# The opening of a GRU kernel: biases by repeating transfers, the first weights in halves, the first x sums on VectorE, and the first pair's products in a held order

## The chip, the cores and the metric

One Trainium2 chip, one core. Times are device microseconds (us); three runs of the kernel before give a median of 2737.33 (2737.08 to 2738.55). One further execution was profiled: 2741.09 us, of which the profile's span is 2739.3. Engines are named as in the profile: PE is TensorE's matmuls, PEld its loading of the stationary operand, DVE is VectorE, ACT is ScalarE, POOL is GpSimd, SP is SyncE, which here only issues transfers.

## What is computed

The input x is 128 rows (batch) by 64 time steps by 512 features, `cond` is 128 by 512. All is float32.

```
gi = x[:, t] @ W_ih + b_ih ;  gh = h @ W_hh + b_hh        # 512 x 1536: groups r, z, n
r = sigmoid(i_r + h_r) ; z = sigmoid(i_z + h_z) ; n = tanh(i_n + r * h_n)
h = (1 - z) * n + z * h                                    # h starts as cond
x = x + h @ (sign-quantized W_ffn).T + b_ffn               # signs scaled by mean |W_ffn|
x = x + moe(conv(x, taps = cond) + b_conv)                 # 64 experts, top 6, and a shared one
```

The change concerns the opening of the first two of these lines; everything behind the 64 recurrent steps is the same in both kernels.

## The kernel before

**Input gates.** `gi` doesn't depend on h, so it is made ahead, two time steps (a *pair*) and 512 output columns (a *group* c: 0 is r, 1 is z, 2 is n) at a time. `input_gates` goes over pairs t = 0, 2, 4, ... and in each over the groups in the order 0, 2, 1. A pair and a group make a `Chunk`. The 2 x 2 block product of a chunk (two steps and two halves of the contraction, two halves by two halves of the weights) is made with seven half-size products, n = 1 to 7, from sums of the blocks instead of eight. Each is two float32 matmuls with 256 columns, and so four rows of the profile (x4, two passes each). Their order in the stream is 1, 6, 7, (3 of the chunk before), 2, 4, 5. Four PSUM banks hold them: psx for 1 and then 2, psy for 6, psw for 7 and then 4, psz for 5 and then 3. After each product VectorE reads the bank (L313 to L327) and adds the parts and the bias `bi`; the bank's next product waits for that.

**Operands.** On the weights' side `prepare(c)` makes four block sums on VectorE, once for each group: t1 (L252), t2 (L254), a difference in place (L255) and t4 (L257). Product 1 needs the first half of the contraction rows of the weight block `wih[c]`, product 6 needs t2, which is made from t1 and the second half. On the input's side `pair_operands(t)` makes four sums of 128 x 256 on GpSimd (L269 to L272) from the pair's tile `xp`.

**Biases.** `b_ih` and `b_hh` come as single rows of 6 KB, laid into spare corners of two later buffers (`xc0`, `tzs[0]`). `spread` (L232) copies a row to all partitions: a matmul with a single row of ones as the stationary operand (L236), for b_ih and b_hh one after the other into one bank, psf, and a ScalarE copy out (L239). `prepare` calls it for each group, and `spread(bhn, ...)` at L403 for the recurrent bias of n. In all six matmuls (twelve rows) and four copies.

**Transfers.** SP issues, in this order: xp of the first pair (L197), the two bias rows (L211, L213), the weight block of group 0 (L215, 1 MB as one transfer), h, the blocks of groups 2 and 1, the three recurrent blocks `whh` (L221), the two repeated rows fb and cb (L222, L223, each a 2 KB row sent to 128 partitions), zero rows, the sign weights' source wf (L408). GpSimd's queue issues the pair t = 2 (L218) and every step's x rows xn (L194); in between are its clearing of the buffer `tzs[0]` (L116) and the sums.

**Recurrence.** The driver takes 24 products off the stream, transposes h (L351, copied out by ScalarE at L357), and makes the signs: sum of |wf| (L411, L415), a matmul that adds over partitions (L417), scale and thresholds (L418 to L422), four times two operations for the signs (L427, L428). Then each step t issues the twelve recurrent matmuls psgh (L441, three groups of four, in the order r, n, z), the gates on VectorE and ScalarE (L448 to L462), the output product of the step before (L375, needs the signs), and 10 or 11 products of the stream, which fill PE while the gates are made.

**What sets the order.** The kernel is written against a scheduler that puts each engine's instructions in a queue by their estimated readiness; a queue runs in order, and an instruction that waits holds all behind it. `tc.issue_after(i)` keeps what is made in its scope behind instruction i on its engine.

Of the kernel before, what the change touches and what calls it, by code (L numbers as in the profile page):

```python
# [1 line left out]

# [6 lines left out]
F32 = mybir.dt.float32  # L9
# [10 lines left out]
P = 128  # L20
B = 128
T = 64
D = 512
KD = D // P
# [18 lines left out]
def adaln_ffn_kernel(  # L43
# [22 lines left out]
    nc = tc.nc  # L66
# [18 lines left out]
        out=before,  # L85
        in_=before,
# [18 lines left out]
    tzs, xcs = [], []  # L105
    cb = conv.enter_context(
        tc.tile_pool(name="cb", bufs=1, side="right", reuse_waits="tile")
    ).tile([P, D], F32, name="cb")

    def conv_buffers(i):  # L110
        cv = conv.enter_context(
            tc.tile_pool(name=f"cv{i}", bufs=1, side="right", reuse_waits="tile")
        )
        tz = cv.tile([P, 2, DS, T], F32, name=f"tz{i}")
        for hf in range(2):
            nc.gpsimd.memset(tz[hf * T : (hf + 1) * T, 1 - hf], 0.0)  # L116
        tzs.append(tz)
        xcs.append(cv.tile([P, B, DS], F32, name=f"xc{i}"))

    conv_buffers(0)  # L120

# [49 lines left out]
    HK = KD // 2  # L171
    HD = D // 2
    gis_ = ExitStack()
    ps_gi = gis_.enter_context(tc.tile_pool(name="ps_gi", bufs=1, space=PSUM))
    with (
# [11 lines left out]
        def load_pair(t, queue=nc.gpsimd):  # L187
            xp = xpp.tile([P, 2, KD, B], F32, name="xp")
            queue.dma_start(out=xp, in_=xT[t : t + 2].rearrange("t p k b -> p t k b"))
            xps[t] = xp  # L190

        def load_x(t):
            xn = io0.tile([P, D], F32, name="xn")
            nc.gpsimd.dma_start(out=xn, in_=x[:, t, :])  # L194
            xns[t] = xn

        load_pair(0, nc.sync)  # L197
        h = el0.tile([P, D], F32, name="h")
# [3 lines left out]
        bhn = w0.tile([P, D], F32, name="bhn")  # L202
        fb = w0.tile([P, D], F32, name="fb")
        scale = w0.tile([P, 1], F32, name="scale")

        bi = w0.tile([P, 3 * D], F32, name="bi")
        wih = [w0.tile([P, KD, D], F32, name=f"wih{c}") for c in range(3)]

        xc0 = xcs[0].rearrange("p b e -> p (b e)")
        bir = xc0[:1, KD * D : (KD + 3) * D]  # L210
        nc.sync.dma_start(out=bir, in_=b_ih.unsqueeze(0))  # L211
        bhr = tzs[0].rearrange("p h c t -> p (h c t)")[:1, : 3 * D]
        nc.sync.dma_start(out=bhr, in_=b_hh.unsqueeze(0))  # L213
        cols = [slice(c * D, (c + 1) * D) for c in range(3)]
        load_rows(wih[0], w_ih[:, cols[0]])  # L215
        nc.sync.dma_start(out=h, in_=cond)
        load_rows(wih[2], w_ih[:, cols[2]])
        load_pair(2)  # L218
        load_rows(wih[1], w_ih[:, cols[1]])
        for c in (0, 2, 1):  # L220
            load_rows(whh[c], w_hh[:, cols[c]])  # L221
        nc.sync.dma_start(out=fb, in_=fbias.partition_broadcast(P))  # L222
        nc.sync.dma_start(out=cb, in_=cbias.partition_broadcast(P))  # L223
        zrow = w0.tile([NPAD, TW], F32, name="zrow")
        nc.gpsimd.memset(zrow, 0.0)
        nc.sync.dma_start(out=tab[NT : NT + NPAD, :], in_=zrow)
# [2 lines left out]
        ones = w0.tile([P, P], F32, name="ones")  # L229
        nc.vector.memset(ones, 1.0)  # L230

        def spread(dst, rows):  # L232

            ps = ps_f.tile([P, D], F32, name="psf")
            for i, row in enumerate(rows):
                nc.tensor.matmul(  # L236
                    ps, ones[:1, :], row, start=(i == 0), stop=(i == len(rows) - 1)
                )
            nc.scalar.copy(dst, ps)  # L239

        wsum = {}

        def prepare(c):

            spread(bi[:, cols[c]], [bir[:, cols[c]]] + ([bhr[:, cols[c]]] if c != 2 else []))
            w = wih[c]
            w11, w12 = w[:, :HK, :HD], w[:, :HK, HD:]
            w21, w22 = w[:, HK:, :HD], w[:, HK:, HD:]  # L250
            t1 = w0.tile([P, HK, HD], F32, name=f"t1{c}")
            nc.vector.tensor_sub(t1, w12, w11)  # L252
            t2 = w0.tile([P, HK, HD], F32, name=f"t2{c}")
            nc.vector.tensor_sub(t2, w22, t1)  # L254
            nc.vector.tensor_sub(w12, w22, w12)  # L255
            t4 = w0.tile([P, HK, HD], F32, name=f"t4{c}")
            nc.vector.tensor_sub(t4, w21, t2)  # L257
            wsum[c] = {1: w11, 2: w21, 3: w22, 4: t4, 5: t1, 6: t2, 7: w12}

        gis = {}  # L260

        def pair_operands(t):
# [6 lines left out]
            nc.gpsimd.tensor_add(s1, x21, x22)  # L269
            nc.gpsimd.tensor_sub(s2, s1, x11)  # L270
            nc.gpsimd.tensor_sub(x21, x11, x21)
            nc.gpsimd.tensor_sub(s4, x12, s2)  # L272
            return {1: x11, 2: x12, 3: s4, 4: x22, 5: s1, 6: s2, 7: x21}

        class Chunk:
# [8 lines left out]
            def product(self, n):  # L284

                name, first = {
                    1: ("psx", True),
                    2: ("psx", False),
                    6: ("psy", True),
                    7: ("psw", True),  # L290
                    4: ("psw", False),
                    5: ("psz", True),
                    3: ("psz", False),
                }[n]
                if first:
                    self.ps[name] = ps_gi.tile([P, D], F32, name=name)[:, :HD]
                ps = self.ps[name]
                for k in range(HK):
                    nc.tensor.matmul(  # L299
                        ps,  # L300
                        self.ops[n][:, k, :],
                        self.ws[n][:, k, :],
                        start=(first and k == 0),
                        stop=(k == HK - 1),
                        skip_group_check=not first,
                    )
                g0, g1 = self.g
                add = nc.vector.tensor_add
                both = ps.unsqueeze(1).to_broadcast([P, 2, HD])
                b = bi[:, cols[self.c]].rearrange("p (h d) -> p h d", h=2)  # L310
                if n == 1:
                    self.p1 = gtp.tile([P, 2, HD], F32, name="p1")
                    add(self.p1, both, b)  # L313
                elif n == 6:
                    self.u2 = gtp.tile([P, 2, HD], F32, name="u2")
                    add(self.u2, both, self.p1)
                elif n == 7:
                    self.u3 = gtp.tile([P, HD], F32, name="u3")
                    add(self.u3, ps, self.u2[:, 1])
                elif n == 5:  # L320
                    add(g1[:, 1], ps, self.u3)
                elif n == 2:
                    add(g0[:, 0], ps, b[:, 0])
                elif n == 4:
                    add(g1[:, 0], ps, self.u2[:, 0])
                elif n == 3:
                    add(g0[:, 1], ps, self.u2[:, 1])  # L327

        def input_gates():


            prev = None
            for t in range(0, T, 2):
                ops = pair_operands(t)
                for c in (0, 2, 1):
                    if t == 0:
                        prepare(c)
                    cur = Chunk(t, c, ops)
                    for n in (1, 6, 7, 3, 2, 4, 5):
                        which = prev if n == 3 else cur  # L340
                        if which:
                            which.product(n)
                            yield
                    prev = cur
            prev.product(3)
            yield
# [53 lines left out]
        for _ in range(24):  # L400
            next(stream)
        hT = transposed(h)
        spread(bhn, [bhr[:, cols[2]]])  # L403

# [25 lines left out]
        for t in range(T):  # L430
            if t + 1 < T:
                load_x(t + 1)
            if t % 2 == 0 and 4 <= t + 4 < T:
                load_pair(t + 4)
            if 2 <= t < 2 * NSL + 2:
                toeplitz(t - 2)
            ps_g = []
            for c in (0, 2, 1):
                ps = ps_gh.tile([P, D], F32, name=f"psgh{c}")
# [7 lines left out]
            r = el0.tile([P, D], F32, name="r")  # L447
            nc.vector.tensor_add(r, ps_r, gis.pop((t, 0)))  # L448
            nc.scalar.activation(r, r, AF.Sigmoid)
            n = el0.tile([P, D], F32, name="n")  # L450
# [17 lines left out]
            h = h_new  # L468
# [48 lines left out]
        nc.vector.tensor_add(xl[:, 1], xl[:, 1], tap[:, 1])  # L517

    conv_buffers(1)
    cb_h = cb.rearrange("p (q h d) -> p q h d", h=2, d=DS)  # L520
    with tc.tile_pool(name="ps_c", bufs=4, space=PSUM) as ps_c:
        for sl in range(NSL):
# [832 lines left out]
```

## Time and profile before

| what | us | where |
|---|---|---|
| median of three runs | 2737.33 | times |
| the profiled execution | 2741.09 | times |
| its span | 2739.3 | page |
| PE busy | 2711.4 (99%) | page, part 1 |
| DVE busy | 1417.0 (52%) | page, part 1 |
| ACT, POOL busy | 428.8, 430.4 (16% each) | page, part 1 |
| first product of the input gates starts | 10.15 | timeline |
| first recurrent matmul starts | 42.24 | timeline |
| moved in the first 60 us | 11.33 MB | DMA view, 0 to 60 us |

How to read it: PE has work nearly all the time, so time is won either by less work on PE or where PE waits. An engine's row gives start, length, operation, output and inputs; brackets at the end give the idle time ahead of it and what ended that.

### The profile page before, as it was taken

The numbers are of one execution on the slowest core, as the hardware profiler recorded it, in microseconds if no ns is written. First come the engines' busy times: TensorE is split into PE (matmuls) and PEld (weight loads), VectorE is DVE, ScalarE is ACT, GpSimd is POOL, SyncE is SP. The second block draws the span as 40 slices with busy tenths as digits, with TensorE's granted clock in tenths as the row PEclk, the third lists the DMA queues.
The fourth block names the chain that finished last, engine by engine and source line by source line (L and its number), as shares of the span: only waits on it lengthen the run. The fifth ranks groups of instructions, "written<-read, shape, count | busy, mean of one in ns | idle before, by whom it ended". The sixth has DMA issues, their size and how long they took to land. (4 is left out here: it accounts for less than half of the span.)

```text
span 2739.3 us, 30134 instructions
## 1 busy us (share of the span) xinstructions
PE 2711.4 (99%) x11459; PEld 1869.4 (68%) x11459; DVE 1417.0 (52%) x3137; ACT 428.8 (16%) x798; POOL 430.4 (16%) x479
## 2 busy tenths in 40 slices
PE   8999999999999999999999999999999999999999
PEld 5666666666666666666669766777776666666667
DVE  5555555555555555555554655655665333333334
ACT  1111111111111111111110222222221111111111
POOL 3111111111211111121110000000001222222120
PEclk9999999999999999999999999999999999999999
DMA  4323331111211111321147641122256898998862
GB/s 166 88 66 77 77 78 50 43 50 43 61 51 43 50 43 50 67 60 50 35 123 220 215 150 20 37 58 55 62 149 184 274 316 242 324 313 259 286 181 47
DMA packets 328164, 326.41 MB, mean 119 GB/s; under 512 B 184274, under 2 KB 250322, under 8 KB 325844
## 3 DMA queue, kind: packets, MB, share of 16 engines
q1 hardware_dynamic: 301092, 252.64, 30.2%
q0 software_dynamic: 26368, 68.17, 10.5%
q10 hardware_dynamic: 560, 3.67, 0.6%
q8 instruction: 91, 1.49, 0.2%
q14 instruction: 53, 0.43, 0.0%
HBM read 238.17 MB, written 94.65 MB: 121 GB/s over the span
## 5 line engine op out<-in xcount | busy, mean ns | idle before, releaser
L441 PE MATMUL psgh<-whh,hT 128*128 128x512 f32 x1536 | 676.2, 596 | 0.7 <-ACT hT L357 0.7
L441 PEld LDWEIGHTS psgh<-whh,hT 128*128 128x128 f32 x1536 | 287.2, 190 | 351.7 <-issue 337.9
L299 PE MATMUL psx<-wih,xp 128*128 128x256 f32 x768 | 199.3, 382 | 1.5 <-DMA wih<-in_w_ih_dram 1.5
L194 POOL DMA_DIRECT2D xn<-in_x_dram x64 | 35.7, 558 | 861.7 <-DVE x L383 861.7
L299 PEld LDWEIGHTS psx<-wih,xp 128*128 128x128 f32 x768 | 144.3, 191 | 23.6 <-issue 4.6
L451 DVE TENSOR_TENSOR n<-psgh,bhn 128x512 f32<-128x512 f32 x64 | 44.3, 692 | 173.4 <-PE psgh L441 172.7
L357 ACT COPY hT<-psf 128x512 f32<-128x512 f32 x64 | 37.5, 586 | 567.8 <-PE psf L351 567.8
L448 DVE TENSOR_TENSOR r<-psgh,gi 128x512 f32<-128x512 f32 x64 | 44.3, 692 | 139.1 <-PE psgh L441 139.1
L157 PE MATMUL psc<-tz,xc 128*128 128x128 f32 x480 | 105.9, 383 | 0.0
L157 PEld LDWEIGHTS psc<-tz,xc 128*128 128x128 f32 x480 | 105.7, 313 | 0.1
L371 POOL TENSOR_TENSOR xn<-xn,fb 128x512 f32<-128x512 f32 x64 | 81.0, 1267 | 154.5 <-DMA xn<-in_x_dram 142.9
L299 PE MATMUL psy<-t,xs 128*128 128x256 f32 x384 | 99.4, 382 | 0.0
L299 PE MATMUL psz<-wih,xs 128*128 128x256 f32 x384 | 98.6, 379 | 0.1
L299 PE MATMUL psz<-t,xs 128*128 128x256 f32 x384 | 98.5, 379 | 0.0
L299 PE MATMUL psw<-t,xp 128*128 128x256 f32 x384 | 98.5, 379 | 0.0
L299 PE MATMUL psw<-wih,xp 128*128 128x256 f32 x384 | 98.5, 379 | 0.0
L375 PE MATMUL psf<-sgn,hhi 128*128 128x512 f32 x256 | 95.2, 493 | 0.0
L1260 PE MATMUL py<-wd,aeT 128*64 128x512 f32 (+1 forms) x384 | 90.6, 601 | 0.0
L1245 DVE SCALAR_TENSOR_TENSOR a<-a,rw,pu 128x352 f32<-128x352 f32 x32 | 18.6, 581 | 136.4 <-PE pu L1236 119.6
L313 DVE TENSOR_TENSOR p<-psx,bi 128x512 f32<-128x512 f32 x96 | 66.4, 692 | 39.5 <-PE psx L299 39.4
L630 PE MATMUL psx<-hid,swg 128*128 128x256 f32 x320 | 83.8, 384 | 1.6 <-DMA swg<-in_sw_gate_dram 1.4
L1270 POOL DMA_INDIRECT out_dram<-ys,idxp x32 | 45.4, 1419 | 250.5 <-ACT ys L1268 192.2
(299 smaller groups left out, 4707.2 us busy)
## 6 DMA issues: line engine op xcount, KB each, us to landing
wg<-in_w_gate_dram SPq DMA_DIRECT2D x64, 704.0 KB
wu<-in_w_up_dram SPq DMA_DIRECT2D x64, 704.0 KB
wd<-in_w_down_dram SPq DMA_DIRECT2D x64, 512.0 KB
xn<-in_x_dram POOLq DMA_DIRECT2D x64, 256.0 KB
xp<-in_xT_dram POOLq DMA_DIRECT2D x31, 512.0 KB
x1c<-x SPq DMA_DIRECT2D x62, 256.0 KB
out_dram<-x SPq DMA_DIRECT2D x62, 256.0 KB
tab<-hid SPq DMA_DIRECT2D x60, 256.0 KB
```

The lines of the kernel that those rows point to most:

```text
L157: i = nc.tensor.matmul(ps[:, j], xcs[sl % 2][:, :, g * 4 + j], tzs[sl % 2][:, :, g * 4 + j, :], start=True, stop=True,)
L299: nc.tensor.matmul(ps, self.ops[n][:, k, :], self.ws[n][:, k, :], start=(first and k == 0), stop=(k == HK - 1), skip_group_check=not first,)
L313: add(self.p1, both, b)
L357: nc.scalar.copy(hT, ps)
L371: nc.gpsimd.tensor_add(xn, xn, fb)
L375: nc.tensor.matmul(ps, piece[:, k, :], sgn[:, k, :], start=(i == 0 and k == 0), stop=(i == 1 and k == KD - 1),)
L441: nc.tensor.matmul(ps, hT[:, k, :], whh[c][:, k, :], start=(k == 0), stop=(k == KD - 1))
L448: nc.vector.tensor_add(r, ps_r, gis.pop((t, 0)))
L451: nc.vector.tensor_add(n, ps_n, bhn)
L630: nc.tensor.matmul(ps.rearrange("p (j b) -> p j b", b=P) if len(r.shape) == 3 else ps, lhs(k), r, start=(first and k == 0), stop=(k == HK ...
L1260: nc.tensor.matmul(py[halves[j]], aeT[:n, c, halves[j]], ws[j][2][:n, c, :], start=(c == 0), stop=(c == len(ech) - 1),)
L1270: nc.gpsimd.indirect_dma_start(out=out, out_offset=bass.IndirectOffsetOnAxis(ap=(idxp[:CAP] if j == 0 else idxo)[:, q : q + 1], axis=0), i ...
```

## The change

- The bias rows are no longer spread by matmuls. `repeated` (a transfer with `partition_broadcast`, 256 KB each in SBUF) brings b_ih of each group straight into `bi`, b_hh of groups 0 and 1 into two tiles and b_hh of n into `bhn`. VectorE adds the second to the first for groups 0 and 1, at the end of `prepare`.
- The first weight block is loaded as two transfers, by contraction halves.
- SP's order is now: xp of the first pair, the two halves, two biases, block 2, its bias, block 1, its two biases, h, xp of the pair t = 2 (on SP now), whh 0, bhn, whh 2, whh 1, fb, cb, zero rows, xn of t = 0 (on SP for t < 3), wf, two more xn.
- The four x sums of the first pair are on VectorE.
- For t = 0 each product is made inside `tc.issue_after` of the last product's matmul. As built, PE's queue starts psx, psy, psw, psx, psw, psz of group 0 (products 1, 6, 7, 2, 4, 5), where before it started psf, psf, psx, psf, psf, psx, psy, psw, psz, with the spreads.
- The clearing of `tzs[0]` is a function of its own, called at t = 1 (and for the second buffer behind its allocation); as built, it stands behind that of zrow in GpSimd's queue.

As built, other instructions move too. On PE, product 5 of the pair t = 2, group 0, is cut in two by the recurrent matmuls, L417 stands ahead of the last two matmuls of the first step's z group instead of behind the first of its r group, and the first step's order on VectorE is: wf's sum, n (L451 before), total, scale, signs, r, z. From the psz product behind the first step's L375 on, PE's order is the same in both kernels.

```diff
+            (nc.sync if t < 3 else nc.gpsimd).dma_start(out=xn, in_=x[:, t, :])
...
-        load_rows(wih[0], w_ih[:, cols[0]])
+        def repeated(dst, row):
+            nc.sync.dma_start(out=dst, in_=row.partition_broadcast(P))
+        for h_ in range(2):
+            half_ = slice(h_ * HD, (h_ + 1) * HD)
+            load_rows(wih[0][:, h_ * HK : (h_ + 1) * HK], w_ih[half_, cols[0]])
+        bh = {}
+        for c in (0, 2, 1):
+            if c:
+                load_rows(wih[c], w_ih[:, cols[c]])
+            repeated(bi[:, cols[c]], b_ih[cols[c]])
+            if c != 2:
+                bh[c] = el0.tile([P, D], F32, name="r")
+                repeated(bh[c], b_hh[cols[c]])
         nc.sync.dma_start(out=h, in_=cond)
-        load_rows(wih[2], w_ih[:, cols[2]])
-        load_pair(2)
-        load_rows(wih[1], w_ih[:, cols[1]])
+        load_pair(2, nc.sync)
         for c in (0, 2, 1):
             load_rows(whh[c], w_hh[:, cols[c]])
+            if c == 0:
+                repeated(bhn, b_hh[cols[2]])
...
         def prepare(c):
-            spread(bi[:, cols[c]], [bir[:, cols[c]]] + ([bhr[:, cols[c]]] if c != 2 else []))
...
             nc.vector.tensor_sub(t4, w21, t2)
+            if c in bh:
+                nc.vector.tensor_add(bi[:, cols[c]], bi[:, cols[c]], bh[c])
...
-            nc.gpsimd.tensor_add(s1, x21, x22)
+            engine = nc.gpsimd if t else nc.vector
+            engine.tensor_add(s1, x21, x22)
...
+                            with tc.issue_after(made[-1].ins) if t == 0 and made else nullcontext():
+                                which.product(n)
...
-        spread(bhn, [bhr[:, cols[2]]])
...
+            if t == 1:
+                clear(0)
```

More of the change, by code (lines that the diff above doesn't have):

```diff
@@ L1 @@
-from contextlib import ExitStack
+from contextlib import ExitStack, nullcontext
 import concourse.bass as bass
@@ L114, in conv_buffers, with clear @@
         tz = cv.tile([P, 2, DS, T], F32, name=f"tz{i}")
-        for hf in range(2):
-            nc.gpsimd.memset(tz[hf * T : (hf + 1) * T, 1 - hf], 0.0)
         tzs.append(tz)
         xcs.append(cv.tile([P, B, DS], F32, name=f"xc{i}"))
+    def clear(i):
+        for hf in range(2):
+            nc.gpsimd.memset(tzs[i][hf * T : (hf + 1) * T, 1 - hf], 0.0)
     conv_buffers(0)
@@ L193, in load_x @@
             xn = io0.tile([P, D], F32, name="xn")
-            nc.gpsimd.dma_start(out=xn, in_=x[:, t, :])
+            (nc.sync if t < 3 else nc.gpsimd).dma_start(out=xn, in_=x[:, t, :])
             xns[t] = xn
@@ L209, in adaln_ffn_kernel @@
         xc0 = xcs[0].rearrange("p b e -> p (b e)")
[L210 to L213, printed above, removed]
         cols = [slice(c * D, (c + 1) * D) for c in range(3)]
-        load_rows(wih[0], w_ih[:, cols[0]])
+        def repeated(dst, row):
[11 more added lines that the diff above has]
+                repeated(bh[c], b_hh[cols[c]])
         nc.sync.dma_start(out=h, in_=cond)
-        load_rows(wih[2], w_ih[:, cols[2]])
-        load_pair(2)
-        load_rows(wih[1], w_ih[:, cols[1]])
+        load_pair(2, nc.sync)
         for c in (0, 2, 1):
             load_rows(whh[c], w_hh[:, cols[c]])
-        nc.sync.dma_start(out=fb, in_=fbias.partition_broadcast(P))
-        nc.sync.dma_start(out=cb, in_=cbias.partition_broadcast(P))
+            if c == 0:
+                repeated(bhn, b_hh[cols[2]])
+        repeated(fb, fbias)
+        repeated(cb, cbias)
         zrow = w0.tile([NPAD, TW], F32, name="zrow")
@@ L230, in adaln_ffn_kernel @@
         nc.vector.memset(ones, 1.0)
[L232 to L239, printed above, removed]
         wsum = {}
         def prepare(c):
-            spread(bi[:, cols[c]], [bir[:, cols[c]]] + ([bhr[:, cols[c]]] if c != 2 else []))
             w = wih[c]
@@ L257, in prepare @@
             nc.vector.tensor_sub(t4, w21, t2)
+            if c in bh:
+                nc.vector.tensor_add(bi[:, cols[c]], bi[:, cols[c]], bh[c])
             wsum[c] = {1: w11, 2: w21, 3: w22, 4: t4, 5: t1, 6: t2, 7: w12}
         gis = {}
+        made = []
         def pair_operands(t):
@@ L268, in pair_operands @@
             s1, s2, s4 = s[:, 0], s[:, 1], s[:, 2]
[L269 to L272, printed above, removed]
+            engine = nc.gpsimd if t else nc.vector
+            engine.tensor_add(s1, x21, x22)
+            engine.tensor_sub(s2, s1, x11)
+            engine.tensor_sub(x21, x11, x21)
+            engine.tensor_sub(s4, x12, s2)
             return {1: x11, 2: x12, 3: s4, 4: x22, 5: s1, 6: s2, 7: x21}
@@ L298, in product @@
                 for k in range(HK):
-                    nc.tensor.matmul(
+                    i = nc.tensor.matmul(
                         ps,
@@ L306, in product @@
                     )
+                made.append(i)
                 g0, g1 = self.g
@@ L341, in input_gates @@
                         if which:
-                            which.product(n)
+                            with tc.issue_after(made[-1].ins) if t == 0 and made else nullcontext():
+                                which.product(n)
                             yield
@@ L519, in adaln_ffn_kernel @@
     conv_buffers(1)
+    clear(1)
     cb_h = cb.rearrange("p (q h d) -> p q h d", h=2, d=DS)
```

## The prediction

> **What bounds the kernel now.** I read the page first, then TensorE's own timeline and the waits of the opening 80 us, then the DMA share by stage, last VectorE's timeline around the first recurrent step.
>
> ```profile
> PE 2711.4 (99%) x11459; PEld 1869.4 (68%) x11459; DVE 1417.0 (52%) x3137; ACT 428.8 (16%) x798; POOL 430.4 (16%) x479
> ```
>
> TensorE is busy 2711.4 of 2739.3 us, so at most some 28 us are to be had from waiting. After 75 us all waits of PE (in the waits view) sum to about 16 us, the longest 2.8, and none is for a line of the change. What the change can reach is the opening:
>
> ```profile
> 4.89 2.04 PE L236 MATMUL psf<-xc,ones 1*128 1x512 f32 x2 [4.89 <-DMA xc<-in_b_ih_dram]
> 6.73 1.91 PE L236 MATMUL psf<-tz,ones 1*128 1x512 f32 x2
> 10.15 2.05 PE L299 MATMUL psx<-wih,xp 128*128 128x256 f32 x4 [1.51 <-DMA wih<-in_w_ih_dram]
> 12.13 2.07 PE L236 MATMUL psf<-xc,ones 1*128 1x512 f32 x2
> 14.87 2.07 PE L236 MATMUL psf<-xc,ones 1*128 1x512 f32 x2 [0.68 <-ACT bi L239]
> 16.87 2.08 PE L299 MATMUL psx<-wih,xp 128*128 128x256 f32 x4
> 18.74 1.83 PE L299 MATMUL psy<-t,xs 128*128 128x256 f32 x4
> 20.41 1.03 PE L299 MATMUL psw<-wih,xp 128*128 128x256 f32 x4
> ```
>
> An x4 row at L299 is one product of the input gates (TensorE's rows alone, with start, length, and the wait ahead). Only two start before 18.7, both psx of group 0. The bias spreads of L236 stand between them in PE's queue: slow ones at 12.13 and 14.87, the latter after a wait for ACT to empty the one psf bank, though what psy needs was there at about 12.3 (t2 ends then). From 20.41 on products follow every 0.863 us.
>
> ```profile
> DVE t L252 <- DMA wih<-in_w_ih_dram: 11.0, 2, 9.0
> PE psf L236 <- DMA xc<-in_b_ih_dram: 4.9, 1, 4.9
> POOL xs L269 <- DMA xp<-in_xT_dram: 2.5, 1, 2.5
> ```
>
> VectorE waits for whole weight blocks: the first has landed at 10.04, the second at 16.09. The DMA engines are not idle meanwhile (the last two columns are DMA share and GB/s):
>
> ```profile
> 4.00:6.00 2.00, 1.11 (x2) 0.62 (x3) 0.00 (x0) 0.00 (x0) 2.00 (x2) 1.00 0.64 215
> 10.00:30.00 20.00, 19.18 (x58) 12.73 (x58) 14.75 (x25) 0.59 (x1) 5.98 (x9) 1.00 1.04 388
> ```
>
> Full from 6 to 30 us. Last, the chain behind the sign weights:
>
> ```profile
> 43.52 0.16 DVE L418 TENSOR_SCALAR scale<-psf 128x1 f32<-128x1 f32 x1 [1.25 <-PE psf L417]
> ...
> 47.00 1.41 DVE L428 SCALAR_TENSOR_TENSOR sgn<-xc,half,r 128x512 fp32r<-128x512 f32 x2
> 48.33 0.68 DVE L448 TENSOR_TENSOR r<-psgh,gi 128x512 f32<-128x512 f32 x1
> ```
>
> From the scale to the first gate VectorE is taken for 4.8 us. Before, this lies under the twelve L441 products (to 52.9) and costs nothing.
>
> **The mark.** As built, the two programs have one order on PE from the psz product that follows the first L375 products, the 38th product in both. Before, it starts at 75.88. The gain is how much earlier it starts; behind it nothing waits long enough to take it back.
>
> **The parts.**
>
> *Bias.* Six spread products and four ACT copies go. The two of row 29.14 and of row 41.19 each held PE for about 1.05 us, 2.1 us in all; the other four make up the opening with its gaps (4.89 to 8.64 and 12.13 to 16.9). In their place come six 256 KB transfers on SP, 1.57 MB; two rows of 6 KB go. At 388 GB/s 256 KB is 0.67 us, which the older repeats (fb, cb, the same form) keep to: fb had landed by 28.30 where POOL started on it. SP's queue is moved accordingly: the pair t=2 and three xn transfers also come from POOL to SP, and each issue there is about 0.4 to 0.6 us, well under the transfer times. Counting bytes in order: second half of block 0 at 9.3, its two biases 10.6, block 2 at 13.3, block 1 at 16.7, its biases 18.0, h 18.7, xp of t=2 at 20.0, the three whh at 22.7, 26.1 and 28.8, wf at 34.2 (fed 32 before). PE asks for blocks 2 and 1 at 16 and 22, xp at 29, h at 32, whh from 35, wf at 35: each is covered, the tightest by about 1 to 3 us, so the extra 1.57 MB costs nothing. If the cover goes, every late microsecond counts in full. Two adds of the bias (DVE, 0.68 like L254) are VectorE work.
>
> *Halves.* The two bias issues ahead of the first block go, so its issue starts at 1.32, not 1.99; all of it should be there 0.67 earlier, at 9.35. The first half holds all of the psx product and t1, estimated at 7 to 7.5; psy needs the second half: t2, 0.68, so psy starts at T0 = 10.1 instead of 18.74; of these 8.6 us the halves and the earlier issue bring the 2.2 below 12.3, the empty queue the rest. Bounds: 8.5 (mean rate without spread of the engines) and 10.0 (no gain from the issue).
>
> *x sums on VectorE.* Four of 128x256. No row has it on VectorE from SBUF; nearest is L323 with 0.42, POOL's L269 is 0.73 above, and half the 0.68 of 512 columns, 0.34, below. 1.5 us from 4.6, or 2.9: over before 9.35 either way, so nothing. The rule that speaks against it is the Trainium skill, SBUF — State Buffer, "two separate sides": a VectorE operation with two SBUF inputs and a GpSimd operation that reads SBUF exclude each other. The trace agrees: L252 takes 680 ns alone and 1486 beside POOL's L271 and L272. By the rule the clearing of tz only writes, so no conflict; were it one, the sums would end at 7.7, still covered. But the rule prices another place: POOL's four sums for t=2 now run near 20 to 23, in VectorE's last preparation (before, they fell into its wait at 13.4 to 16.8). I take 0.75 us; 0 if they miss, 1.5 if they hit twice.
>
> *Held order.* After the first psx group 0 now goes psy, psw, psx, psw, psz, so that the second psx, which waits until VectorE has read the first with the bias, stands behind two products. It adds no operation; on PE's queue only products stand behind the held ones. VectorE has 5.9 us for a group with preparation (five at 0.60, two at 0.61, five at 0.34 from start to start), PE 6.04; with the POOL block PE waits about 1.0 us in the stretch, bounds 0.3 and 1.7.
>
> *Clock.* The Trainium skill, TensorE: Matmul & The Clock Gate, "What's actually happening", says some 3.4 us of sustained activity open the clock. By it the spreads, PE work from 4.9 to 8.6 and in the run from 10.1 to 14.2, would have served, and dropping them would make three products cold, 2.5 us. The rows say otherwise: the psx at 16.87 is still slow (2.08), and only 3.5 us of full-size products later, at 20.41, is a product 1.03; the spreads use one row. (The granted clock column shows 1.00 throughout.) So the loss is nothing: psy and psw are slow at 1.71 each, as psx and psy were.
>
> *Clearing of tz* moves on POOL behind zrow and to no one's path; 0, and with it the bias wait in xc goes.
>
> **The sum.** From psy to the mark, 36 products: 2 x 1.71 + 34 x 0.863 = 32.75; two transposes 0.87; 24 L441 products, 2 x 9.98 = 19.96; L417 0.42; L375 2.24: 56.25. Waits: 1.0 in preparation. Then one that is new: as built, VectorE has n (L451 before) and total behind the second psgh, and scale, signs, r and z follow before it reads the psz result. Psgh are through at 45.5; fillers last 3 us; psz is free only after 4.8 + 0.6 + 0.6 + 0.4 from the scale at 44.2, so PE stops about 2.0, with two later stops of 0.36: 2.7 (bounds 0, if PE's fillers last, and 4, if POOL's xn additions of L371, 1.27 each, fall on the sign steps). hT 0.2. In all 10.1 + 56.25 + 3.9 = 70.25, 5.6 earlier than 75.88. The profiled execution takes 2741.09 (span 2739.3, 1.8 around it) and would take 2735.5; it stands 3.76 above the median 2737.33, so the forecast is 2737.33 - 5.6 = **2731.7**.
>
> **Rivals.** (1) This forecast, gain 4.5 to 6.6: 0.48; over 0.2% (5.5 us), what a measurement can tell, in 0.29. (2) The stop behind the signs is shorter or absent and the half lands by 8.5: 5.6 + up to 2.7 gives 6.6 to 8.4, 2729 to 2731; for it speaks the DMA share of 0.64 at 4 to 6, room that the earlier issue can use; against it the order of VectorE's queue. 0.30. (3) Transfers are late, all 15% slower than counted, or the second half at 10: the mark at 71 to 72.5, gain 3 to 4.5, 2733 to 2734.3; for it, an opening rate of 215 GB/s. 0.19. (4) Slower: the repeating reads of one 2 KB row are slow. Eight lie ahead of wf, whose slack is 5.8 us against the second psgh at 42 less the 2.3 of L411; at 0.67 + d each the delay is 8d - 5.8, equal to the gain at d = 1.4, and 0.2% slower from d = 2.1, 2748 at 3. Fb and cb speak against it. 0.03. That the halves or the order don't happen is excluded by the built order.
>
> Faster by over 0.2%: 0.29 + 0.30 = 0.59; slower 0.03; within 0.38. The range leaves out the ends of (2) and (3): 2728.9 to 2734.2.
>
> **What would show it.** First product at about 7, second at 10 and no psx of group 2 before five more; products of 1.03 from 13.5; psgh from about 35; PE stopping near 49 for the psz buffer; the mark near 70.3. Wrong: psy past 11, PE waiting for a whh block, or L411 starting after 40.

## The result, and the profile after

The changed kernel takes 2730.95 us (median of 14 runs, 2729.61 to 2733.55), the kernel before 2738.33 (14 runs beside them, 2736.1 to 2741.66). The ratio is 0.9972, 95% interval 0.9965 to 0.9979: 0.28% faster, 7.4 us between the medians. The profiled execution takes 2733.45, its span is 2731.6, 7.7 less than before. The mark, the first psz product behind the first output product, starts at 68.91 instead of 75.88: 6.97 of those 7.7 us are won before it. In every kernel below 37 products precede the mark, and TensorE's order behind it is the same; yet from the mark to the end of the span the profiled executions, one for each kernel, take from 2659.5 to 2665.0 us. So the fine comparisons are made at the mark, and the medians stand beside it. Before, on TensorE's timeline:

```profile
42.24 1.12 PE L441 MATMUL psgh<-whh,hT 128*128 128x512 f32 x2
...
75.88 1.03 PE L299 MATMUL psz<-wih,xs 128*128 128x256 f32 x4
```

TensorE's busy time has gone down by 6.6 us, nearly as much as the span, since the spreads counted as busy:

```profile
PE 2704.8 (99%) x11447; PEld 1866.4 (68%) x11447; DVE 1413.4 (52%) x3143; ACT 426.1 (16%) x794; POOL 425.6 (16%) x471
```

After, TensorE's timeline of the opening (start, length, operation, and in brackets the wait ahead and what ended it):

```profile
6.05 2.05 PE L308 MATMUL psx<-wih,xp 128*128 128x256 f32 x4 [6.05 <-DMA wih<-in_w_ih_dram]
8.29 2.07 PE L308 MATMUL psy<-t,xs 128*128 128x256 f32 x4 [0.19 <-DVE t L259]
10.16 1.26 PE L308 MATMUL psw<-wih,xp 128*128 128x256 f32 x4
11.85 1.13 PE L308 MATMUL psx<-wih,xp 128*128 128x256 f32 x4 [0.43 <-DVE p L323]
13.17 1.13 PE L308 MATMUL psw<-t,xp 128*128 128x256 f32 x4 [0.19 <-DVE u L329]
...
34.07 8.75 PE L454 MATMUL psgh<-whh,hT 128*128 128x512 f32 x20
```

Nothing but products stands in the opening. The first waits for the first half of the block, the second (psy) for VectorE's t2 at 8.29, not 18.74. Only two products are slow; the third already takes 1.26. The recurrent matmuls start at 34.07 instead of 42.24. VectorE waits for the weights once, 0.8 us, in place of twice for 11.0 (waits of the first 80 us: total, times, longest):

```profile
DVE t L259 <- DMA wih<-in_w_ih_dram: 0.8, 1, 0.8
```

The DMA engines are full at 4 to 6 us, two microseconds sooner, and after 10 us as full as before (stretch, busy time by engine, granted clock, DMA share, GB/s):

```profile
4.00:6.00 2.00, 0.00 (x0) 0.00 (x0) 1.35 (x4) 0.00 (x0) 1.95 (x2) 1.00 1.02 386
...
10.00:30.00 20.00, 19.19 (x83) 15.26 (x83) 16.95 (x32) 0.00 (x0) 5.20 (x5) 1.00 1.04 389
```

Between 6 and 10 us they move less than before (253 GB/s against 348), so that over the first 10 us the two kernels move about the same (232 and 235 GB/s). What is gained is not rate: the block now comes first. Last the sign chain, VectorE's timeline:

```profile
42.97 0.16 DVE L429 TENSOR_SCALAR scale<-psf 128x1 f32<-128x1 f32 x1 [1.01 <-PE psf L428]
...
43.54 0.88 DVE L438 TENSOR_SCALAR r<-xc,nhalf 128x512 f32<-128x512 f32 x2
44.33 1.41 DVE L439 SCALAR_TENSOR_TENSOR sgn<-xc,half,r 128x512 fp32r<-128x512 f32 x2
...
47.78 0.68 DVE L461 TENSOR_TENSOR r<-psgh,gi 128x512 f32<-128x512 f32 x1
48.38 0.68 DVE L469 TENSOR_TENSOR z<-psgh,gi 128x512 f32<-128x512 f32 x1
48.98 0.41 DVE L331 TENSOR_TENSOR gi<-psz,u 128x256 f32<-128x256 f32 x1
```

The signs take VectorE from 42.97 to 47.78, r and z follow, and only at 48.98 is the psz bank read, for which TensorE has stopped (its timeline, with the mark):

```profile
49.53 1.10 PE L308 MATMUL psz<-wih,xs 128*128 128x256 f32 x4 [1.76 <-DVE gi L331]
...
68.91 1.02 PE L308 MATMUL psz<-wih,xs 128*128 128x256 f32 x4
```

### The profile page after: what moved, and what is told of

It is laid out like the page before. It is cut to its first block, busy times and chain, and to the rows that moved or that the text cites. A ratio compares the mean times of both kernels' runs of the same rounds, so it can differ in the third digit from the quotient of the medians.

```text
span 2731.6 us, 30112 instructions
## 1 busy us (share of the span) xinstructions
PE 2704.8 (99%) x11447; PEld 1866.4 (68%) x11447; DVE 1413.4 (52%) x3143; ACT 426.1 (16%) x794; POOL 425.6 (16%) x471
## 3 DMA queue, kind: packets, MB, share of 16 engines
q0 software_dynamic: 25984, 66.86, 10.6%
## 4 chain that ended last, share of the span: by engine, by line
PE 95%; DMA 2%; issue 2%; DVE 1%; ACT 0%; SPq 0%; DVEq 0%; POOLq 0%; ACTq 0%
PE psgh L454 24%; PE psw L644 7%; PE psz L644 6%; PE psx L644 6%; PE psw L308 6%; PE psz L308 6%; PE psx L308 6%; PE psf L387 4%; PE psc L159 4%; PE py L1274 3%; PE y L644 3%; PE psy L308 3%; PE pg L1250 3%; PE pu L1250 3%; PE y L818 2%
## 5 line engine op out<-in xcount | busy, mean ns | idle before, releaser
L644 PE MATMUL psx<-xr,swg 128*128 128x256 f32 x320 | 84.3, 385 | 0.0
```

The costliest lines, as they stand in the source:

```text
L644: nc.tensor.matmul(ps.rearrange("p (j b) -> p j b", b=P) if len(r.shape) == 3 else ps, lhs(k), r, start=(first and k == 0), stop=(k == HK ...
```

## The experiments

All twelve kernels compute the whole of the reference. Ratios are against the kernel before on the same chip, with 95% intervals. Three chips were used for the twelve, and the median of the kernel before went from 2738.33 to 2740.96 in these comparisons; so read the ratios, and don't subtract medians of different rows. In each timeline the line numbers are that kernel's own.

| kernel | mark | first psgh | profiled | median | ratio |
|---|---|---|---|---|---|
| before | 75.88 | 42.24 | 2741.09 | 2738.33 | |
| after | 68.91 | 34.07 | 2733.45 | 2730.95 | 0.9972 (0.9965 to 0.9979) |
| 1 one-row spreads back | 77.90 | 44.23 | 2741.73 | 2742.61 | 1.0008 (0.9999 to 1.0016) |
| 2 first block whole | 67.29 | 33.68 | 2732.47 | 2731.15 | 0.9960 (0.9946 to 0.9973) |
| 3 x sums on GpSimd | 68.36 | 34.14 | 2732.45 | 2731.28 | 0.9963 (0.9949 to 0.9976) |
| 4 no held order | 67.88 | 33.02 | 2729.85 | 2730.79 | 0.9964 (0.9950 to 0.9977) |
| 5 one-row spreads of repeated biases | 76.67 | 43.02 | 2740.47 | 2737.66 | 0.9989 (0.9981 to 0.9998) |
| 6 the same, full height | 73.95 | 37.96 | 2736.45 | 2735.37 | 0.9988 (0.9981 to 0.9995) |
| 7 before, repeated biases alone | 72.81 | 38.39 | 2739.59 | 2737.62 | 0.9990 (0.9984 to 0.9997) |
| 8 the same, and held | 77.80 | 43.38 | 2742.26 | 2741.16 | 1.0006 (0.9999 to 1.0012) |
| 9 after less 2, 3 and 4 | 68.64 | 35.02 | 2729.84 | 2732.40 | 0.9976 (0.9967 to 0.9985) |
| 10 sign weights loaded earlier | 71.40 | 34.68 | 2734.51 | 2734.51 | 0.9980 (0.9972 to 0.9988) |
| 11 the same, not held | 69.46 | 33.16 | 2735.22 | 2733.87 | 0.9979 (0.9971 to 0.9987) |
| 12 as 9, GpSimd's queue as before | 73.26 | 41.01 | 2736.51 | 2736.22 | 0.9990 (0.9982 to 0.9998) |

**1. The spreads back.** The changed kernel with the bias rows (6 KB each) and the one-row spreads in place of the repeating transfers.

```diff
-            repeated(bi[:, cols[c]], b_ih[cols[c]])
...
+            spread(bi[:, cols[c]], [bir[:, cols[c]]] + ([bhr[:, cols[c]]] if c != 2 else []))
```

> The changed kernel with the biases spread again by one-row matmuls (two 6 KB rows, six spreads, four copies), all its other parts kept. Theory A (the gain is mostly PE's queue freed of the spreads): the spreads stand again among the first products, slow, and two more hold PE about 1.05 us each later; psy may still start near 8.5, but the mark (psz behind the first L375 products) goes from 68.9 back to 72 to 74; time 3 to 5 us over the changed kernel, 2734 to 2736. Theory B (the halves, the sums on VectorE and the held order carry it): the mark stays below 71, time within 2 us of the changed kernel.

The whole gain went, and more than I had expected: the mark at 77.90, not 72 to 74. TensorE's timeline says why:

```profile
10.18 0.59 PE L314 MATMUL psw<-wih,xp 128*128 128x256 f32 x2
10.71 1.12 PE L249 MATMUL psf<-xc,ones 1*128 1x512 f32 x2
...
14.24 2.07 PE L249 MATMUL psf<-xc,ones 1*128 1x512 f32 x2 [0.68 <-ACT bi L252]
16.25 2.08 PE L314 MATMUL psx<-wih,xp 128*128 128x256 f32 x4
...
25.53 1.74 PE L314 MATMUL psx<-wih,xp 128*128 128x256 f32 x4
27.11 1.03 PE L314 MATMUL psy<-t,xs 128*128 128x256 f32 x4
```

Half a product takes 0.59 and a one-row spread 1.12 near 10 to 11: the clock has opened, as in the kernel after. At 14.24 the same spread takes 2.07, and full-size products are slow again until 27.11, though TensorE has no gap from 14.24 on. The windows view of the same kernel has the granted clock in its third column from the end:

```profile
9.91:13.31 3.40, 3.40 (x10) 1.28 (x9) 0.00 (x0) 0.00 (x0) 0.00 (x0) 1.00 1.05 394
13.32:13.57 0.25, 0.25 (x1) 0.00 (x0) 0.00 (x0) 0.00 (x0) 0.00 (x0) 0.50 1.02 385
...
14.00:27.00 13.00, 12.76 (x22) 6.89 (x23) 6.49 (x12) 1.36 (x3) 2.91 (x4) 0.50 1.05 389
```

The clock opens at 9.90 and closes at 13.32. Between the two TensorE is busy without a gap, so the stop of 0.68, which only begins at 13.57, did not close it; some 2.0 of these 3.4 us are one-row spreads. Then TensorE is busy for 12.76 of 13 us at half its clock. The spreads don't just use time; the clock closes over them. Experiments 5 and 6 separate this from the change of transfers.

**2, 3, 4. One of the other parts undone.** First the block in one transfer:

```diff
-        for h_ in range(2):
-            half_ = slice(h_ * HD, (h_ + 1) * HD)
-            load_rows(wih[0][:, h_ * HK : (h_ + 1) * HK], w_ih[half_, cols[0]])
+        load_rows(wih[0], w_ih[:, cols[0]])
```

> The changed kernel with the first weight block as one transfer again. Theory A: the block still ends at about 7.5, t1 and t2 follow it, psy starts near 8.9 instead of 8.3, and the second psx is held by the bias as before (r lands at 10.2): mark 68.9 to 69.5, loss 0 to 0.6 us, 2731 to 2731.6. Theory B: psy goes back by the 2 us between the two halves' landing, loss 1.5 to 2.5 us, 2732.5 to 2733.5.

then the x sums of the first pair on GpSimd:

```diff
-            engine = nc.gpsimd if t else nc.vector
+            engine = nc.gpsimd
```

> The changed kernel with the first pair's four x sums on GpSimd again. If GpSimd's reading sums shut VectorE's two-input sums out (as L252 at 1486 ns beside them suggests): they run from about 6.1, behind the clearing of tz, to 9.0, t1 cannot start before about 8 to 9, the first bank is read near 12.4 and the mark comes 1.0 to 1.6 us later, about 70.2. If they don't: s2 is there at 7.6, psy unchanged, loss 0 to 0.3 us.

then the products free of the held order:

```diff
-                            with tc.issue_after(made[-1].ins) if t == 0 and made else nullcontext():
-                                which.product(n)
+                            which.product(n)
```

> The changed kernel without the held order: as built, half of product 5 stands ahead of psy in PE's queue and splits the later psz products; the bias and transfers are as in the changed kernel. Theory A: half a product (slow, 0.85 us) falls into PE's wait between 8.1 and 8.3 and delays psy by 0.5 to 0.7, but the second psx waits for the bias in any case: loss 0 to 0.4 us, mark 68.9 to 69.3. Theory B: the order matters, loss over 1 us.

None of the three loses anything at the mark: 67.29, 68.36 and 67.88 against 68.91, earlier than I had expected of any of them, and the intervals of the ratios overlap that of the whole change. The prices are partly there in the timelines, but they are made up elsewhere. With the whole block psy starts 1.2 later, at 9.49. In the kernel after, TensorE slips by 0.95 in all between 18 and 28 us; in this build it does not, and the recurrent matmuls start 0.4 earlier. The sum over partitions also stands earlier on TensorE, and the stop near 48 is 0.52 instead of 1.76. With the sums on GpSimd two preparation steps take 1.21 instead of 0.68, and the second psx and psw wait 0.79 and 0.88; the conflict with GpSimd near 22 is there as well (1.10 and 0.88), but TensorE no longer slips behind it. So no one of these three parts carries the gain by itself.

**5 and 6. Does a one-row matmul count for the clock?** Both kernels keep the repeating transfers and the queues of the changed kernel, but the repeated biases are copied through TensorE as before: by one row of ones, or by 128 rows of 1/128, which gives the same sum with as many columns and instructions. The edit from 5 to 6, without the constant:

```diff
-                    ps, lone[:1, :], row[:1], start=(i == 0), stop=(i == len(rows) - 1)
+                    ps, lone[:128, :], row[:128], start=(i == 0), stop=(i == len(rows) - 1)
```

> The changed kernel with its repeating transfers kept, but landing in spare corners and spread from there by six one-row matmuls and four ScalarE copies, as before; nothing else differs from its twin e6_full_spread than that here one row of the stationary operand and one of the moving one are used. Theory A (one-row matmuls don't open TensorE's clock, and let it close): products around the spreads are slow (2.05) until well after 15 us, mark 74 to 77. Theory B (the slow products of e1_spread come from its 0.68 us stop and the waits alone): products are fast from 13 on, mark 72 to 73, as in the twin.

> The twin with full-height matmuls: the same number of matmuls with the same columns in the same queue order, the stationary operand 128 rows of 1/128 and the moving one all 128 repeated rows (the sum gives the same bias). Theory A: the clock opens by 12 and stays open; the spreads take 0.86 to 1.05 each and the mark comes 3 to 6 us before that of e5_row_spread, at 70 to 72. Theory B: no difference from e5_row_spread beyond 0.5 us.

One row (TensorE's timeline of 5):

```profile
16.03 2.07 PE L256 MATMUL psf<-xc,lone 1*128 1x512 f32 x2
18.03 2.08 PE L321 MATMUL psx<-wih,xp 128*128 128x256 f32 x4
...
21.61 1.30 PE L321 MATMUL psz<-t,xs 128*128 128x256 f32 x4
22.75 1.03 PE L321 MATMUL psx<-wih,xp 128*128 128x256 f32 x4
```

Full height (of 6):

```profile
11.24 1.85 PE L256 MATMUL psf<-tz,lone 128*128 128x512 f32 x2
12.93 0.60 PE L321 MATMUL psy<-t,xs 128*128 128x256 f32 x2
13.37 1.03 PE L321 MATMUL psw<-wih,xp 128*128 128x256 f32 x4
```

Same work in the same order, and the fast products begin near 13 in one and near 22 in the other; the recurrent matmuls start 5.1 us apart, the marks 2.7 (kernel 6 has two later stops, 0.90 and 0.60). The mark of 6 was expected at 70 to 72; it came at 73.95. The medians, 2737.66 and 2735.37, lie in the same direction, but the ratios don't separate the two. That one-row matmuls don't count is shown by the rows, not by the time. Even at full height the spreads cost 5.0 us at the mark against the kernel after.

**7 and 8. The biases alone.** The kernel before with repeating biases in place of the rows and spreads, and nothing else; then the same with the held order.

```diff
-            spread(bi[:, cols[c]], [bir[:, cols[c]]] + ([bhr[:, cols[c]]] if c != 2 else []))
...
+            if c in bh:
+                nc.vector.tensor_add(bi[:, cols[c]], bi[:, cols[c]], bh[c])
```

> The kernel before with the repeating transfers and the bias adds alone (whole first block, sums and the pair t=2 on GpSimd, no held order, the clearing in its old place). As built, PE's queue then has psx of group 2 ahead of psy of group 0, and VectorE's queue a preparation of group 1 ahead of the reading of psy. Theory A (the spreads' absence is enough): mark 68.5 to 70, time as the changed kernel. Theory C (the other parts are what keeps the queues in an order that can use it): psx of group 2 waits for block 2 at about 16.5, the reading of psy for block 1 at about 20, the mark is 71 to 73.5, so 2.5 to 5 us of the 7.4 us gain stay.

> e7_bias_alone with the held order of the first pair's products. PE's queue is in order again but for the transposes of h, which stand ahead of psy; VectorE's queue has the whole preparation of groups 2 and 1 ahead of the reading of psy, so it waits for block 1. Theory A: mark 68.5 to 70. Theory C: psw's second product waits for VectorE until about 21, mark 72.5 to 74.5, gain 1.5 to 3.5 us: the hold alone is worth nothing without earlier operands.

The biases alone bring 3.1 us at the mark (72.81) and 0.1% in time: the spreads have to go, but that is not enough. As built, group 2's first psx stands ahead of group 0's psz and psy on TensorE, and psy starts only at 20.33; on VectorE the preparation of block 2 and t1 of block 1 stand ahead of reading it. Holding TensorE's order on top puts the mark at 77.80, later than before the change and than either theory had it. TensorE's timeline of 8:

```profile
14.93 1.03 PE L303 MATMUL psx<-wih,xp 128*128 128x256 f32 x4
23.81 2.07 PE L303 MATMUL psw<-t,xp 128*128 128x256 f32 x4 [7.85 <-DVE u L324]
```

TensorE's queue is in the wanted order, but VectorE's still has t1 of block 1, landed near 20, ahead of reading psy, and TensorE stops for 7.85; the clock closes over it (granted 0.56 from 23 to 29 us). An order held on one engine only moves the stop if the engine that frees its banks keeps another order.

**9. All three undone together.** If 2, 3 and 4 stand in for one another, taking away all three must show it.

> The changed kernel with three of its parts undone together: the first block is one transfer, the x sums of the first pair are on GpSimd, no product is held. The repeating bias transfers and the moved transfers stay. As built, TensorE starts psx, psz, psy, psw, psx of group 0 and then half of group 2's psy, ahead of group 0's last psw; VectorE has t1 of block 2 ahead of reading the first psy. Theory A (the three parts stand in for each other, and one of them is needed to keep the queues in order): the early psy of group 2 and the early t1 wait for block 2, which lands near 13; TensorE stops once for 1 to 2 us near 14, the clock may close over it, and the mark (the first psz after the first output product) comes at 70 to 72, 2735 to 2737 profiled. Theory B (with the spreads gone, none of the three is needed at all): the mark is at 67 to 69 as in each of the single undoings, 2730 to 2733. Theory C (they are needed jointly and badly, as the biases alone at 72.8): 72.5 to 74, 2738 to 2740.

The mark is at 68.64. The theory that one of the three is needed (70 to 72) fell at the mark. In the opening the three together are worth 0.95: the recurrent matmuls start at 35.02 instead of 34.07, with the expected stop near 14. A shorter stop at the signs, 0.53 instead of 1.76, gives it back: in this build the sum over partitions stands earlier on TensorE (41.89 instead of 42.65), so a later stage hides the loss:

```profile
12.93 1.03 PE L306 MATMUL psx<-wih,xp 128*128 128x256 f32 x4
14.97 0.67 PE L306 MATMUL psy<-t,xs 128*128 128x256 f32 x2 [1.02 <-DVE t L257]
...
49.26 1.10 PE L306 MATMUL psz<-wih,xs 128*128 128x256 f32 x4 [0.53 <-DVE gi L329]
```

What 9 has and 7 has not is: h loaded behind block 1, the pair t = 2 and three xn tiles on SP, and the clearing of `tzs[0]` behind the first sum in GpSimd's queue. The last two are told apart from h by the next run.

**12. GpSimd's queue as before.** Kernel 9 with that queue put back:

```diff
+    clear(0)
...
-            (nc.sync if t < 3 else nc.gpsimd).dma_start(out=xn, in_=x[:, t, :])
+            nc.gpsimd.dma_start(out=xn, in_=x[:, t, :])
...
+            if c == 1:
+                load_pair(2)
...
-        load_pair(2, nc.sync)
...
-            if t == 1:
-                clear(0)
```

> The kernel of the run with three parts undone, and GpSimd's queue put back as it was before the change: the clearing of the buffer stands ahead of the first x sums, and the pair t=2 and the x rows are issued by GpSimd again (the pair between the blocks 2 and 1). The biases repeat, and h stays behind block 1. It lies between the biases alone (mark 72.8) and the three parts undone (68.64), and differs from the biases alone mainly in the place of h. As built, both psx of group 0 come first, then group 2's psx, and only then psz and psy; VectorE has t1 of block 1 ahead of reading the first psy. Theory A (GpSimd's queue, which sets when the first x sums are there, is what the three parts stood in for): psy starts at 15 to 19, reading it waits for block 1, which lands near 16 to 17, TensorE stops 2 to 4 us in the opening, and the mark comes at 71.5 to 73.5; 2736.5 to 2739 profiled, median about 2735 to 2737.5. Theory B (the early h and its transposes made the biases alone lose): the mark stays at 68 to 70, 2731 to 2733.5 profiled.

The mark moved from 68.64 to 73.26, 4.6 us, as the first theory had it (though psy came later and TensorE stopped longer than it said), and the ratio from 0.9976 to 0.9990. The place of h, all that is left between 7 and 12, makes no gain (72.81 and 73.26). TensorE's timeline:

```profile
7.57 2.04 PE L308 MATMUL psx<-wih,xp 128*128 128x256 f32 x4 [7.57 <-DMA wih<-in_w_ih_dram]
14.18 2.08 PE L308 MATMUL psx<-wih,xp 128*128 128x256 f32 x4 [4.56 <-DVE p L323]
16.77 2.07 PE L308 MATMUL psx<-wih,xp 128*128 128x256 f32 x4 [0.52 <-DVE gi L333]
18.64 1.91 PE L308 MATMUL psz<-t,xs 128*128 128x256 f32 x4
...
21.20 1.41 PE L308 MATMUL psy<-t,xs 128*128 128x256 f32 x4
```

and VectorE's:

```profile
8.95 2.57 DVE L259 TENSOR_TENSOR t<-wih,t 128x512 f32<-128x512 f32 x1
```

Psy's operands are there at 11.5 (t2 ends then; GpSimd's four sums end at 10.96, where kernel 9 has them at 10.2). It starts at 21.20 because two more psx, a psz and half a psx stand ahead of it. The second psx waits 4.56 until VectorE, busy with preparation, has read the first, and the third 0.52 until it has read the second; all are slow. The sums end only 0.7 later than in 9, but they now fall on the preparation: t1 and t2 take 1.46 and 2.57 beside them (1.06 and 1.10 in 9), and VectorE reads the first psx at 13.43 instead of 12.08. So some 1.35 of the 4.56 is this conflict, and the rest the place of the second psx, which in 9 stands behind psz, psy and psw. The transfers move with the queue: blocks 2 and 1 have landed at 14.62 and 18.96 instead of 12.91 and 16.30, but TensorE waits for neither. That the scheduler made this order because it counts the clearing (3.65 us) and the DMA issues ahead of the sums is my reading of the two built orders, and not shown; which of the two it is was not run, nor was the changed kernel with only GpSimd's queue put back, where the sums are on VectorE.

**10 and 11. A version that beats both?** The stop of 1.76 at the signs should go if the sign weights' source lands earlier, ahead of the last recurrent block; 11 also drops the held order.

```diff
+            if c == 1:
+                wf = xc0[:, : KD * D].rearrange("p (k o) -> p k o", k=KD)
+                load_rows(wf, wfT)
```

> The changed kernel with the load of the sign weights' source moved ahead of the last recurrent block on SP. As built, the sum over partitions then stands behind the first recurrent matmul instead of the tenth, and the scale and the four sign steps come on VectorE before the first step's gates. Theory A (the stop of 1.76 near 49 is the sign chain's place in VectorE's queue, and the load order decides it): the source lands near 29 to 31, the last recurrent block near 36 (used from about 41), the sign steps lie under the recurrent matmuls, the stop is under 0.5, and the mark comes at 66.5 to 67.7 instead of 68.9; 2731 to 2732.3 profiled, median 2729 to 2730.5. Theory B (something else ends that stop: the reading of the product banks by the gates): the stop stays at 1.3 to 2.2 and the mark at 68.3 to 69.5, no gain. Against both: if the last block lands after 41, TensorE waits for it and each late microsecond is lost.

> As the run before, and no product held to the order of its operands. With the products not held the mark came 1.0 earlier (67.87) than with them. Theory A (the two act at different places, the opening and the sign chain): the gains add, mark 65.5 to 66.8, 2728 to 2730 profiled, median 2727.5 to 2729.5. Theory B (not holding gained by moving the same sign chain): they do not add, and the mark is at 66.8 to 68, median 2729 to 2731.

Both theories of 10 fell, and both of 11. The source landed in time and no block was late, but the marks are 71.40 and 69.46, later than the 68.91 of the kernel after. VectorE's timeline of 10:

```profile
36.46 1.88 DVE L439 TENSOR_SCALAR r<-xc,nhalf 128x512 f32<-128x512 f32 x2
38.27 2.34 DVE L440 SCALAR_TENSOR_TENSOR sgn<-xc,half,r 128x512 fp32r<-128x512 f32 x2
40.53 2.89 DVE L439 TENSOR_SCALAR r<-xc,nhalf 128x512 f32<-128x512 f32 x2
43.34 2.41 DVE L440 SCALAR_TENSOR_TENSOR sgn<-xc,half,r 128x512 fp32r<-128x512 f32 x2
...
50.38 0.41 DVE L334 TENSOR_TENSOR gi<-psz,u 128x256 f32<-128x256 f32 x1
```

and GpSimd's:

```profile
40.02 4.52 POOL L386 TENSOR_TENSOR xn<-xn,fb 128x512 f32<-128x512 f32 x3
```

The rows of the sign steps add up to 9.5 us instead of 4.6, since they now run beside GpSimd's x sums (from 36.48) and xn additions, which in the kernel after were over at 42.4, before the signs began. The last step shows it: it begins when GpSimd has finished (44.54), and takes 0.74, as in the kernel after; the seven before it are all slower. Then r, the whole of n and z stand ahead of reading psz (50.38; in the kernel after only r and z), and TensorE stops 2.51. Behind the stop the clock closes (TensorE's timeline of 10, and its windows, laid on the times at which the granted clock changes in this trace):

```profile
50.94 1.45 PE L311 MATMUL psz<-wih,xs 128*128 128x256 f32 x4 [2.51 <-DVE gi L334]
52.18 1.91 PE L311 MATMUL psx<-wih,xp 128*128 128x256 f32 x4
```

```profile
48.15:51.56 3.41, 0.90 (x5) 0.60 (x4) 2.71 (x6) 1.26 (x2) 0.00 (x0) 1.00 0.00 0
51.56:54.97 3.41, 3.41 (x10) 2.65 (x9) 2.72 (x6) 0.00 (x0) 0.00 (x0) 0.50 0.00 0
```

In the first stretch TensorE works for 0.90 of 3.41 us; in the second the granted clock is 0.50, and three products take 4.35 us instead of 2.59, 1.76 more. The mark of 10 is 2.49 later than that of the kernel after. Without the held order (11) the stop is longer, 2.87, but the clock stays open; its windows, laid the same way:

```profile
44.89:48.30 3.41, 1.98 (x10) 1.39 (x8) 2.58 (x5) 1.26 (x2) 0.00 (x0) 1.00 0.00 0
48.30:51.72 3.42, 1.97 (x8) 1.44 (x8) 3.42 (x7) 0.63 (x1) 0.00 (x0) 1.00 0.00 0
```

The gain of about 1.5 in the opening (first psgh 33.16 against 34.68) doesn't become a new best. None of the versions I ran is measurably faster than the change itself; 2, 3 and 4 are about as fast.

## Why the prediction was right, and where not

**Time.** 2731.7 was forecast, 2730.95 measured, within the range. That the two are only 0.8 apart is partly luck: the forecast was counted from 2737.33, and beside the changed kernel the one before took 1.0 more, so the gain was 7.4 where 5.6 was forecast. At the mark it was 6.97, outside the 4.5 to 6.6 of the likeliest case. What happened is one half of the second case: the half landed before 8.5, but the stop at the signs was no shorter.

**The mis-sized term: "all of it should be there 0.67 earlier, at 9.35".** By the landing records in the trace the first half had landed at 5.91 and the second at 7.44, and psy started at 8.29, not at T0 = 10.1. This 1.8 is more than the whole error of the mark (1.34). I had taken the issue's 0.67 from the 10.04 of before, as though the rate stayed. The DMA share at 4 to 6 us went from 0.64 to 1.02. It is not the halves that did it: with the block in one transfer and no bias rows ahead of it (kernels 2, 7, 8, 9 and 12) the first product starts at 7.56 to 7.66, so the block has landed by then, against 10.04 behind the two 6 KB rows. Taking those two short transfers from the head of the queue was worth 2.4 us. How much of this is the issue and how much the rows' own packets was not separated.

**From psy to the mark** I had 60.15; it was 60.62. In the stretch in which the weights are prepared it came to about 0.7 more than counted, net: psy took 1.87 from start to start, not 1.71, the second psx waited 0.43 for the bias, the two products behind it started 0.6 late, and TensorE slipped by another 0.95 between 18 and 28; the clock, opening at 10.62, gave 0.45 back (psw took 1.26, not 1.71). The bias transfer was in time (landed at 10.21, counted 10.6), but the add stands behind it, and psy was earlier than counted. The stop at the signs was 1.76 by its row, not about 2.0, and the two later stops came as slow starts (1.11 and 1.20 from start to start instead of 0.863): some 2.6 us in all, as counted (2.7).

**Bias.** That the spreads did nothing for the clock was right, and 5 against 6 shows it. That their cost is their own time was too little: in 1 the clock opened and closed again over them, which makes the loss 9.0 at the mark, more than the change gained. The 1.57 MB more cost nothing, as predicted: TensorE waited for no whh block. Wf came at 36.24, not 34.2, but the steps behind its sum had to wait for a recurrent product until 41.14 in any case.

**Halves, sums, hold.** The attribution was wrong. I gave the halves and the earlier issue 2.2 of the 8.6 at psy, and let the held order keep the second psx away. Each of the three can go, and all three together, without a loss at the mark (2, 3, 4, 9), though for all three together that is luck: 0.95 is lost in the opening and won back at the signs. The sums cost nothing on VectorE (0.42 each, from 4.62 to 6.17), as predicted, but they are not needed there either.

**"Clearing of tz moves on POOL behind zrow and to no one's path; 0".** This step failed in its reason. With the three parts undone, GpSimd's queue, that is the clearing together with the issues of the pair t = 2 and xn, is worth 4.6 us (9 against 12). Nobody waits for the clearing itself, but with the queue the built order of psx, psz and psy changes, and the sums move onto VectorE's preparation. "The empty queue" of the sum was not a consequence of dropping the spreads; in 7 and 12 the place is taken by group 2's psx.

**SBUF conflict.** The 0.75 for GpSimd's sums of t = 2 was sound: on VectorE two steps beside them took 1.04 and 1.21 instead of 0.68, 0.89 more.

**Rivals.** Late transfers and slow repeated reads did not occur: block 2 landed at 12.94, block 1 at 16.32, the three whh at 22.81, 26.20 and 28.91, within 0.4 of what was counted. In the fourth rival two sums were off: from wf at 34.2 the slack is 5.5, not 5.8, and d = 3 gives 2750, not 2748; neither bears on the forecast.

## What to carry to other kernels

Where a scheduler orders the queues by estimated readiness, cost an edit by the built order of every engine, GpSimd's included: a clearing and a few transfer issues on GpSimd were worth 4.6 us here (with three parts undone), though TensorE waited for none of them directly. Take away one part at a time and then all the small ones together before crediting any; at the mark three of the parts were each without effect, and so were all three. Look at more than one place in the timeline when you do, since a later stop can hide an earlier loss. And before moving a load earlier, look at what the released work will then run beside: the sign steps doubled from 4.6 to 9.5 us beside GpSimd.

## What the runs showed of the hardware

- One-row matmuls did not count for TensorE's clock. In 1 it closed at 13.32 behind 3.4 us without a gap, of which some 2.0 were one-row, and stayed closed until 26.97 though TensorE had no gap from 14.24 on; in 5 fast products came only after some 4 us of full-height ones. The Trainium skill, TensorE: Matmul & The Clock Gate, "What's actually happening", lets activity open the clock and an idle window of about 3.4 us close it; the 7.85 stop of 8 agrees, but in these runs one-row work counted as idle. From where full-height work sets in to the opening it took 3.5 (before) to 6.7 us (kernel 6).
- In these traces the granted clock changes only at times a whole number of 3.41 us apart: in 1 at 9.90, 13.32 and 26.97, in 8 at 14.64, 18.05 and 28.29, in 10 at 10.60, 51.56 and 54.97. So where a stop falls on this grid counts as much as its length: the 2.51 of 10 lies in one stretch of 3.41, with 0.90 of work in it, and closed the clock; the 2.87 of 11 lies over two, with 1.98 and 1.97, and did not. How much work keeps it open is not settled: near 1519 us of the kernel after it closed behind a stretch with 2.46 us of other matmuls.
- The granted clock column shows a clock that closes again (0.50 in 1, 0.56 in 8), but not the slow one before the first opening (1.00 for the kernel after from 6 to 10 us, for 5 from 8 to 22): there only the length of equal matmuls tells.
- A VectorE step can lose to several GpSimd steps in a row: t2 took 2.57 beside three sums in 7, 8 and 12, against 0.68 alone. The Trainium skill, SBUF — State Buffer, "two separate sides", has the two exclude each other, for a VectorE operation with two SBUF inputs or in a 2-port mode. The one-input sign step of 10 suffered as well (2.89 for two, 0.88 alone). That alone it takes 0.48 for 512 columns, where a two-input sum takes 0.68, would fit such a mode; no row shows the mode itself.
- Two 6 KB rows at the head of a queue held the 1 MB block behind them back: before, the first of its 16 shares had landed at 6.93 and the last at 10.01, by the landing records; without them (kernel 2) it was 7.00 and 7.52.
